# Moving the next to last node batch, and parts of the last one, in the tail of a graph network kernel

## The chip, the cores and the metric

The kernel runs on one core of a Trainium2 chip. A core has five engines, each with its own queue of instructions: TensorE (PE in the profile; its weight loads are listed as PEld), VectorE (DVE), ScalarE (ACT), GpSimd (POOL) and SyncE (SP). They tell each other of finished work by semaphores. Data moves by DMA. Direct transfers are issued by SP, a few by ScalarE; gathers by an index are issued by POOL. The metric is the device time of one execution in microseconds, and lower is better.

## The reference

One layer of a graph network on 6250 nodes with 128 features, and 100000 edges that are sorted by destination. For each edge, the features of both its ends and 4 features of its own go through a small network; its results are summed for each destination node; each node is then updated from its own features and its sum, with two normalizations at the end.

```python
msg_in = concatenate([x[src], x[dst], edge_features], axis=1)
h = silu(msg_in @ mW1 + mb1)
messages = h @ mW2 + mb2
aggregated = segment_sum(messages, dst, num_segments=6250)
u = silu(concatenate([x, aggregated], axis=1) @ uW1 + ub1)
updated = u @ uW2 + ub2
out = layernorm(x + layer_norm(x + updated, ln_g, ln_b))
```

## The kernel before

**Tables.** The first stage multiplies all nodes by the two halves of mW1 and writes two tables to memory, tab_a for sources and tab_b for destinations, so that an edge needs only to add one row of each.

**Groups of edges.** The 100000 edges are cut into 98 groups (NG, numbered 0 to 97) of 1024 (8 tiles of 128); the last group has 6 tiles. For each group g:

- `fetch(g)` has POOL gather the rows of tab_a, one indirect DMA for each tile (line 277), into a buffer ga (six of them). A gather can be made to wait for instructions that are given as further arguments: the first of them holds the first tile, the second the fifth tile. In the steady part these are `begun[g + 2]`, the first matmul of the group's own `products`, and `summing[g]`, the first matmul of the sums of the group two before.
- `load(g)` has SP load 96 rows of tab_b (mv) and the edges' own features (into st).
- `products(g)` makes, on TensorE, the destination part of the first layer in PSUM (pre, line 623).
- `hidden(g)` adds ga and pre on VectorE (s, line 640), and applies Silu on ScalarE (h, line 641).
- `by_nodes(g)` multiplies h by a matrix of zeros and ones, oh (line 609), on TensorE, and so sums the edges of each of 96 nodes in PSUM (pt, line 652).
- `add(g)` adds pt to the sums of all nodes in acc (line 665), and for every fourth group the counts of edges in deg (line 670).

**Batches of nodes.** Sorted edges mean that early nodes are complete before later groups are read. `node_batch` updates four tiles of nodes at a time, as a Python generator: each `yield` ends a step, and `advance` takes every running batch one step further, so that the batches' instructions are strewn among the groups'. The steps are: load x (xs, line 495) and copy the sums; products (y, lines 510, 511 and 515); Silu (uT, line 518); products (lines 521 and 530); residual sum and moments (lines 532, 483 and 484); square root (r, line 489); z and its moments (lines 542 and 545); square root; shift; scaling (line 560); store (line 564). The next to last batch has three tiles of nodes and begins in group 95. The last batch, `final`, has two; it adds the biases to xs early (lines 507 and 508), reads acc and deg directly, and takes its buffers from the pool of the gathers' buffers.

**What sets the order.** The order of each engine's queue is the order in which the Python code issues instructions; nothing is rearranged (the schedule is manual). Semaphore waits are derived from the data. Lines 680 to 722 are the loop over groups: in group g it issues `hidden(g)`, `products(g + 2)`, the matrices of later groups, `by_nodes(g)`, a fetch, adds, and then steps of the batches (line 721: four calls in each of groups 95 and 96). Lines 724 to 759 are the tail: group 97 in two pieces of four and two tiles (`piece`, lines 731 to 734), with `final` around it. A small activation at line 748 ("primed") brings Silu's table back to ScalarE ahead of the pieces, since square root and Silu need different tables.

Of the kernel before, what the change touches and what calls it, by code (L numbers as in the profile page):

```python
# [8 lines left out]
F32 = mybir.dt.float32  # L9
I32 = mybir.dt.int32  # L10
U8 = mybir.dt.uint8
AF = mybir.ActivationFunctionType
# [6 lines left out]
P = 128  # L19
# [5 lines left out]
def kernel(  # L25
# [40 lines left out]
    nc = tc.nc  # L66
    N, H = x.shape
# [4 lines left out]
    G = 8  # L72
    GE = G * P
    NG = -(-E // GE)
# [5 lines left out]
    CLOSE = 14  # L80
# [5 lines left out]
    BT = 4  # L86
# [91 lines left out]
    ones = consts.tile([P, P], F32, name="ones")  # L178
# [94 lines left out]
    def fetch(g, *after):  # L273

        rows[g] = gath.tile([P, G, H], F32, name="ga")
        for i in range(tiles_of(g)):
            ins = nc.gpsimd.indirect_dma_start(  # L277
                out=rows[g][:, i, :],
                out_offset=None,
                in_=x if g < RAW else tab_a[:, :],  # L280
                in_offset=bass.IndirectOffsetOnAxis(
                    ap=src_i[:, g, i : i + 1] if g else src_0[:, i : i + 1], axis=0
                ),
            )
            part, at = divmod(i * len(after), G)
            if after and at == 0 and after[part]:
                tc.add_manual_dep(
                    ins.ins,
                    after[part].ins.name,
                    mybir.DependencyInfo(  # L290
                        mybir.DependencyClass.Sync, mybir.DependencyReason.DATA
                    ),
                    reason="TensorE keeps up with the gathers",
                )
# [124 lines left out]
    def rows_ps():  # L419
        return ps.tile([P, G, P], F32, name="pre")  # L420
# [45 lines left out]
    def node_batch(i0, n, work, new, y, final=False):  # L466

        cols = slice(i0 * P, (i0 + n) * P)
        m = (min((i0 + n) * P, N) - i0 * P) // n
        assert m * n == min((i0 + n) * P, N) - i0 * P  # L470

        def rows_of(t):

            return t[i0 * P : i0 * P + m * n].rearrange("(p j) f -> p j f", j=n)

        def flat(t):
            return t[:, :n].rearrange("p i f -> p (i f)")

        def moments(v):
            mv = work.tile([P, BT, 2], F32, name="mv", bufs=2)  # L480
            for i in range(n):
                st = work.tile([P, 6], F32, name="st", bufs=2)
                nc.vector.bn_stats(st, v[:, i, :])  # L483
                nc.vector.bn_aggr(mv[:, i, :], st)
            return mv

        def std(mv):
            r = work.tile([P, BT], F32, name="r", bufs=2)
            nc.scalar.activation(r[:, :n], mv[:, :n, 1], AF.Sqrt, bias=eps)  # L489
            return r  # L490

        xs = new("xs")
        if m < P:
            nc.vector.memset(xs[m // 32 * 32 :, :n], 0.0)
        nc.sync.dma_start(xs[:m, :n], rows_of(x))
        sums, counts = acc[:, cols], deg[:, cols]
        if not final:

            acc_b, deg_b = new("acc_b"), new("deg_b", DR)
            nc.scalar.copy(flat(acc_b), sums)  # L500
            nc.scalar.copy(flat(deg_b), counts)
            sums, counts = flat(acc_b), flat(deg_b)
        yield
        xb = xs
        if final:
            xb = new("xb")
            nc.vector.tensor_add(xb[:, :n], xs[:, :n], b_b[:, None, :].to_broadcast([P, n, H]))
            nc.vector.tensor_add(xs[:, :n], xs[:, :n], ub2_b[:, None, :].to_broadcast([P, n, H]))
        y = y()
        nc.tensor.matmul(flat(y), u1x, xT[:, cols], start=True, stop=False)  # L510
        nc.tensor.matmul(flat(y), mb2u, counts, start=False, stop=False)  # L511
        if final:

            yield
        nc.tensor.matmul(flat(y), w2u, sums, start=False, stop=True)  # L515
        yield
        uT = new("uT")
        nc.scalar.activation(flat(uT), flat(y), AF.Silu, bias=ub1_col)  # L518
        yield
        if not final:  # L520
            nc.tensor.matmul(  # L521
                y[:, :n],
                ones[0:1, :],
                ub2_row[:, None, :].to_broadcast([1, n, H]),
                start=True,
                stop=False,
            )
        by_p = flat(uT).rearrange("k (p j) -> k p j", j=n)
        for i in range(n):
            nc.tensor.matmul(y[:, i, :], by_p[:, :, i], u2, start=final, stop=final or i == n - 1)  # L530
        yield
        nc.vector.tensor_add(y[:, :n], y[:, :n], xs[:, :n])  # L532
        mv = moments(y)
        if not final:
            nc.vector.tensor_add(xs[:, :n], xs[:, :n], b_b[:, None, :].to_broadcast([P, n, H]))
        yield
        r = std(mv)
        yield
        nc.vector.reciprocal(r[:, :n], r[:, :n])
        z = new("z")  # L540
        for i in range(n):
            nc.vector.scalar_tensor_tensor(
                y[:, i, :], y[:, i, :], mv[:, i, 0:1], g_b, op0=OP.subtract, op1=OP.mult
            )
            nc.vector.scalar_tensor_tensor(
                z[:, i, :], y[:, i, :], r[:, i : i + 1], xb[:, i, :], op0=OP.mult, op1=OP.add
            )
        mz = moments(z)
        yield
        rz = std(mz)  # L550
        yield
        nc.vector.reciprocal(rz[:, :n], rz[:, :n])
        shift = work.tile([P, BT], F32, name="shift", bufs=2)
        nc.vector.scalar_tensor_tensor(
            shift[:, :n], mz[:, :n, 0], -1.0, rz[:, :n], op0=OP.mult, op1=OP.mult
        )
        yield
        o = z
        for i in range(n):
            nc.scalar.activation(  # L560
                o[:, i, :], z[:, i, :], AF.Identity, bias=shift[:, i : i + 1], scale=rz[:, i : i + 1]
            )
        yield
        (nc.scalar if final else nc.sync).dma_start(rows_of(out), o[:m, :n])
# [4 lines left out]
    def advance(running):  # L569

        for b in list(running):
            if next(b, running) is running:
                running.remove(b)
# [106 lines left out]
    for g in range(NG):  # L680
        if g == 1:
            load_weights()
        if g == 2:
            running.append(destination_checks(node_y()))
        if g == 8:
            running.append(fuse_weights())
        for c in range(1, NC):
            if g == max(1, c * EC // GE - 10):
                attributes(c)
            if g == max(1, c * EC // GE - 10) + 1:  # L690
                attribute_rows(c)
        if g + LEAD < NG:
            load(g + LEAD)
        last = g >= NG - 1
        if not last:
            h[g] = hidden(g)
        if g + 2 < NG:
            pre[g + 2] = products(g + 2)
        if g + MADE < NG:
            node_matrix(g + MADE)  # L700
        if g + 1 < NG:
            oh[g + 1] = edge_matrix(g + 1)
        if g - 2 in pt:
            add(g - 2, pt.pop(g - 2))
        if last:
            break
        pt[g] = by_nodes(g, h.pop(g), oh.pop(g))
        if CLOSE <= g + 2 < NG:
            fetch(g + 2, begun[g + 2], summing[g])
        elif g == 0:  # L710
            fetch(7, ended[1], begun[2])
        elif g == 1:
            fetch(8, begun[3], summing[1])
        elif g % 2:
            fetch(g // 2 + 8, ended[g + 1], begun[g + 2] if g == CLOSE - 3 else ended[g + 2])
        if g >= NG - 3:
            add(g - 1, pt.pop(g - 1))
        for i0, n, first in batches[:-1]:
            if g == (first if first >= NG - 3 else first + 1):
                running.append(node_batch(i0, n, *node_tiles(nodes, node_y)))  # L720
        for _ in range(4 if g >= NG - 3 else 2 if g >= NG - 6 else 1):
            advance(running)

    g = NG - 1
    n = tiles_of(g)
    ga, pg, oh_g, h_g = rows.pop(g), pre.pop(g), oh.pop(g), hbuf[g % NH]
    s = work.tile([P, G, H], F32, name="s")
    primed = consts.tile([1, 1], F32, name="primed")
    before = running.pop()

    def piece(lo, hi):
# [1 line left out]
        nc.scalar.activation(h_g[:, lo:hi], s[:, lo:hi], AF.Silu)  # L733
        sums(g, pt[g], h_g, oh_g, lo, hi)

    final = node_batch(
        *batches[-1][:2],
        nodes,

        lambda name, p=P: gath.tile([P, G, H], F32, name="ga")[:p, :BT],  # L740
        lambda: rows_ps()[:, :BT],
        final=True,
    )
    while running:
        advance(running)
    next(final)

    nc.scalar.activation(primed, ones[0:1, 0:1], AF.Silu)
    add(g - 1, pt.pop(g - 1))
    pt[g] = degrees(g)  # L750
    next(final)
# [165 lines left out]
```

## Time and profile before

| what | us |
|---|---|
| median of 3 runs | 1178.11 (1177.94 to 1178.4) |
| profiled execution | 1179.78 |
| its span, first to last instruction | 1177.7 |
| busy: PE, POOL | 747.7, 743.2 |
| busy: PEld, DVE, ACT | 675.3, 486.4, 238.9 |

The profile is of one execution. "Busy" is the time in which an engine works, so that waiting for a semaphore is not in it. In a line of the timeline the columns are start and duration in us, engine, line of the kernel, operation, output and inputs, shapes, how many instructions are merged in the line, and in brackets the idle time before it with what ended it ("remote" is a release that the profile doesn't put down to an instruction). Matmul ends are modelled. An fp32 matmul shows as two records. In a line of the chain of waits the columns are start, duration, and what the time went to. In a group's line stand line, engine, operation and names, then the number of instructions, busy us, mean ns of one, and the idle time before them with its cause.

### The profile page before, as it was taken

The page shows a single profiled execution, that of the slowest core. Times are in us where ns is not written, and L with a number is a line of the kernel's source. Part 1 is how long each engine was busy: PE and PEld are TensorE (multiplying, and loading weights), DVE is VectorE, ACT ScalarE, POOL GpSimd, SP SyncE. Part 2 cuts the span into 40 slices and gives each one's busy share as a digit, 9 for nine tenths or more (in the row PEclk, how much of TensorE's full clock was granted, in tenths as well). Part 3 has the DMA queues.
Part 4 walks back from the last instruction along what each step waited for, and adds up shares of the span by engine and source line. Part 5 has one row for each costly group of instructions (what it writes and reads, how often), then busy time and mean ns, then how long its engine had stood idle before and what let it go on. Part 6 is the DMA issues. An engine that isn't in the chain of part 4 may idle for free.

```text
span 1177.7 us, 11313 instructions
## 1 busy us (share of the span) xinstructions
PE 747.7 (63%) x3645; PEld 675.3 (57%) x3645; DVE 486.4 (41%) x1017; ACT 238.9 (20%) x297; POOL 743.2 (63%) x790
## 2 busy tenths in 40 slices
PE   5776896656756666567647666656566565656654
PEld 4575786555655656465646565555565464656533
DVE  4461654433532523532533353342343252353344
ACT  2211121220321311120221121121132131122132
POOL 6646666665666666666666666666666666656660
PEclk9877877676565666567566667666666667667665
DMA  8762232222222221222222213221222222212110
GB/s 198 203 156 71 75 85 65 67 82 61 74 66 73 67 72 52 79 72 73 55 72 76 58 57 81 65 81 56 71 74 66 71 74 63 65 55 69 47 59 20
DMA packets 70076, 89.01 MB, mean 76 GB/s; under 512 B 20703, under 2 KB 51694, under 8 KB 70010
## 3 DMA queue, kind: packets, MB, share of 16 engines
q0 software_dynamic: 25024, 51.30, 15.8%
q1 hardware_dynamic: 40408, 35.03, 10.3%
q10 hardware_dynamic: 4578, 1.89, 0.7%
q8 instruction: 31, 0.51, 0.2%
q14 instruction: 35, 0.29, 0.1%
HBM read 76.78 MB, written 11.38 MB: 75 GB/s over the span
## 4 chain that ended last, share of the span: by engine, by line
PE 35%; issue 32%; POOL 20%; DVE 2%; DMA 1%; another core or an unknown queue 1%; ACT 1%; DVEq 0%; POOLq 0%; SPq 0%; ACTq 0%
POOL ga L277 20%; PE pre L623 17%; PE pt L652 14%; PE pre L626 1%; PE y L530 1%; DMA ga<-tab_a,src_i 1%; PE y L521 1%; PE y L510 1%; PE y L511 0%; PE y L515 0%; DVE s L640 0%; DVE st L483 0%; DVE oh L609 0%; PE pt L647 0%
## 5 line engine op out<-in xcount | busy, mean ns | idle before, releaser
L277 POOL DMA_INDIRECT ga<-tab_a,src_i x742 | 703.7, 948 | 384.2 <-issue 187.1
L623 PE MATMUL pre<-mv,st 100*128 100x128 f32 x1564 | 345.1, 396 | 229.5 <-issue 199.5
L623 PEld LDWEIGHTS pre<-mv,st 100*128 100x128 f32 x1564 | 315.2, 301 | 248.4 <-issue 224.3
L652 PE MATMUL pt<-oh,h 128*128 128x96 f32 x1564 | 293.7, 348 | 147.6 <-issue 143.8
L652 PEld LDWEIGHTS pt<-oh,h 128*128 128x128 f32 x1564 | 279.9, 266 | 165.8 <-issue 162.3
L640 DVE TENSOR_TENSOR s<-ga,pre 128x1024 f32<-128x1024 f32 x92 | 112.2, 1220 | 502.6 <-DMA ga<-tab_a,src_i 419.8
L641 ACT ACTIVATE h<-s 128x1024 f32<-128x1024 f32 x92 | 97.1, 1056 | 671.5 <-issue 409.6
L596 DVE TENSOR_SCALAR_CACHE_REDUCE st<-near,p_next 96x1024 f32<-96x1024 uint8 x98 | 124.3, 1270 | 2.9 <-DMA near<-near_d 1.5
L609 DVE TENSOR_TENSOR oh<-w_row,rel 128x768 f32<-128x768 f32 x98 | 93.0, 949 | 42.5 <-remote 42.2
L277 POOL DMA_INDIRECT ga<-in_x_dram,src_i x32 | 30.7, 960 | 16.4 <-issue 8.8
L532 DVE TENSOR_TENSOR y<-y,xs 128x512 f32<-128x512 f32 (+1 forms) x12 | 8.3, 688 | 74.4 <-issue 70.7
L641 ACT ACT_TABLE_LOAD x23 | 29.5, 1283 | 24.2 <-PE pre L626 17.6
L489 ACT ACT_TABLE_LOAD x24 | 30.8, 1283 | 6.1 <-DVE st L483 5.7
L377 PE MATMUL wide<-w,xT 128*128 128x256 f32 x98 | 27.6, 441 | 3.5 <-DVE x_sb L380 3.5
L665 DVE TENSOR_TENSOR acc<-acc,pt 128x96 f32 x98 | 23.7, 242 | 12.5 <-PE pt L652 7.7
L530 PEld LDWEIGHTS y<-u,uT 128*128 128x128 f32 x94 | 22.7, 326 | 10.7 <-issue 10.7
L518 ACT ACTIVATE uT<-y,ub_col 128x512 f32<-128x512 f32 (+1 forms) x12 | 8.1, 678 | 96.5 <-remote 83.6
L377 PEld LDWEIGHTS wide<-w,xT 128*128 128x128 f32 x98 | 21.5, 227 | 8.3 <-DVE x_sb L380 4.3
L530 PE MATMUL y<-u,uT 128*128 128x128 f32 x94 | 25.4, 423 | 0.0
L670 DVE TENSOR_TENSOR deg<-deg,pt 1x96 f32 x98 | 24.4, 249 | 1.0
L626 PE MATMUL pre<-w,ga 128*128 128x128 f32 x80 | 19.4, 326 | 2.7 <-issue 2.6
L521 PE MATMUL y<-ub_row,ones 1*128 1x512 f32 (+1 forms) x24 | 15.5, 729 | 6.9 <-ACT uT L518 6.9
(118 smaller groups left out, 361.7 us busy)
## 6 DMA issues: line engine op xcount, KB each, us to landing
ga<-tab_a,src_i POOLq DMA_INDIRECT x742
near<-near_d SPq DMA_DIRECT2D x24, 384.0 KB
mv<-tab_b SPq DMA_DIRECT2D x98, 48.0 KB
tab_a<-t SPq DMA_DIRECT2D x6, 512.0 KB
tab_b<-x_sb SPq DMA_DIRECT2D x6, 512.0 KB
xs<-in_x_dram SPq DMA_DIRECT2D x11, 256.0 KB
out_dram<-z SPq DMA_DIRECT2D x11, 256.0 KB
st<-ea_d SPq DMA_DIRECT2D x98, 16.0 KB
```

What stands on the lines that cost most here:

```text
L277: ins = nc.gpsimd.indirect_dma_start(out=rows[g][:, i, :], out_offset=None, in_=x if g < RAW else tab_a[:, :], in_offset=bass.IndirectOffs ...
L377: ins = nc.tensor.matmul(pm[:, j], xT[:, cols], w1, start=True, stop=True)
L489: nc.scalar.activation(r[:, :n], mv[:, :n, 1], AF.Sqrt, bias=eps)
L521: nc.tensor.matmul(y[:, :n], ones[0:1, :], ub2_row[:, None, :].to_broadcast([1, n, H]), start=True, stop=False,)
L530: nc.tensor.matmul(y[:, i, :], by_p[:, :, i], u2, start=final, stop=final or i == n - 1)
L596: nc.vector.tensor_scalar(stbuf[g % NST][:W], near.pop(g), p_next, 0.0, op0=OP.is_equal, op1=OP.add, accum_out=deg_q[g // DQ % 2][:, g % D ...
L609: nc.vector.tensor_tensor(oh, w_row[:, None, :].to_broadcast([P, G, W]), rel[:, g, :, None].to_broadcast([P, G, W]), op=OP.is_equal,)
L623: ins = nc.tensor.matmul(pre[:, i, :], st[:, i, :], mv[g % NM], start=True, stop=g >= RAW)
L626: ins = nc.tensor.matmul(pre[:, i, :], rows[g][:, i, :], w1[:, 0, :], start=False, stop=True)
L640: nc.vector.tensor_add(s[:, :n], ga[:, :n], ps[:, :n])
L641: nc.scalar.activation(h[:, :n], s[:, :n], AF.Silu)
L652: ins = nc.tensor.matmul(pt[:, :W], h[:, i, :], oh[:, i, :], start=i == 0, stop=i == tiles_of(g) - 1)
```

## The change

There are three parts.

1. In group 96 the four steps of the next to last batch are issued at the head of the group, ahead of `hidden(96)`, and no longer at its end.
2. `final` is made at the end of group 95 and takes its first step there (memset and load of xs). Its second step is issued at the end of group 96; a new `yield` ends this step after the first product (line 510), and the product with the counts (line 511) follows with group 97 after its `degrees`. The small activation at line 748 is gone.
3. The six gathers of group 97 are issued by `fetch(g + 2)` without further arguments, so they don't wait for `begun[97]` and `summing[95]`. All other groups keep theirs.

```diff
         nc.tensor.matmul(flat(y), u1x, xT[:, cols], start=True, stop=False)
+        if final:
+            yield
         nc.tensor.matmul(flat(y), mb2u, counts, start=False, stop=False)
 ...
         last = g >= NG - 1
+        if g == NG - 2:
+            for _ in range(4):
+                advance(running)
         if not last:
             h[g] = hidden(g)
 ...
-        if CLOSE <= g + 2 < NG:
+        if CLOSE <= g + 2 < NG - 1:
             fetch(g + 2, begun[g + 2], summing[g])
+        elif g + 2 == NG - 1:
+            fetch(g + 2)
 ...
-        for _ in range(4 if g >= NG - 3 else 2 if g >= NG - 6 else 1):
+        for _ in range(0 if g == NG - 2 else 4 if g == NG - 3 else 2 if g >= NG - 6 else 1):
             advance(running)
+        if g == NG - 3:
+            final = node_batch(
+                *batches[-1][:2],
+                nodes,
+                lambda name, p=P: gath.tile([P, G, H], F32, name="ga")[:p, :BT],
+                lambda: rows_ps()[:, :BT],
+                final=True,
+            )
+            next(final)
+        if g == NG - 2:
+            next(final)
 ...
-    primed = consts.tile([1, 1], F32, name="primed")
 ...
-    final = node_batch(
-        ...
-    )
     while running:
         advance(running)
-    next(final)
-
-    nc.scalar.activation(primed, ones[0:1, 0:1], AF.Silu)
     add(g - 1, pt.pop(g - 1))
     pt[g] = degrees(g)
     next(final)
```

More of the change, by code (lines that the diff above doesn't have):

```diff
@@ L734, in piece @@
         sums(g, pt[g], h_g, oh_g, lo, hi)
-    final = node_batch(
[L737 to L742, printed above, removed]
-    )
     while running:
         advance(running)
-    next(final)
-    nc.scalar.activation(primed, ones[0:1, 0:1], AF.Silu)
     add(g - 1, pt.pop(g - 1))
```

## The prediction

> **What bounds the kernel now.** I read the page from top to bottom, then the chain of waits and the timeline of the last 60 us, because the change begins in group 95 of 0 to 97.
>
> ```profile
> span 1177.7 us, 11313 instructions
> PE 747.7 (63%) x3645; PEld 675.3 (57%) x3645; DVE 486.4 (41%) x1017; ACT 238.9 (20%) x297; POOL 743.2 (63%) x790
> ...
> L277 POOL DMA_INDIRECT ga<-tab_a,src_i x742 | 703.7, 948 | 384.2 <-issue 187.1
> ```
>
> No engine is full. Most of the run is the gathers' rhythm: one starts every 1.25 us (0.95 busy, 0.30 idle), and now and then POOL stands still until TensorE reports. The change leaves all that alone up to about 1137 us. What follows is a tail, and the chain of waits tells what sets it:
>
> ```profile
> 1138.37 7.42 another core or an unknown queue
> ...
> 1145.87 0.59 ACT uT L518
> 1146.46 0.04 issue
> 1146.50 1.64 PE y L521 x2
> 1148.14 1.59 PE y L530 x6
> ...
> 1156.08 2.08 DMA ga<-in_x_dram
> ...
> 1160.58 2.89 PE pt L652 x12
> ```
>
> The chain runs through the next to last node batch, then the load of the last batch, then the two pieces of group 97. The 7.42 us without a name are the largest single piece. The timeline shows what they are:
>
> ```profile
> 1139.13 0.48 PE L515 MATMUL y<-acc_b,w2u 128*128 128x384 f32 x1 [1.03 <-issue]
> ...
> 1145.80 0.26 DVE L665 TENSOR_TENSOR acc<-acc,pt 128x96 f32 x1 [4.80 <-remote]
> 1145.82 0.94 POOL L277 DMA_INDIRECT ga<-tab_a,src_i  x1 [2.46 <-remote]
> 1145.87 0.58 ACT L518 ACTIVATE uT<-y,ub_col 128x384 f32<-128x384 f32 x1 [7.50 <-remote]
> ```
>
> TensorE's last product of that batch ends at 1139.61 by its record. VectorE, GpSimd and ScalarE all wait for TensorE (for pt of group 95, for its first product, for y), and all three start within 0.07 us at 1145.8. So TensorE's signals come up to 6 us later than its records, in one burst. The timeline of POOL gives a hint on when:
>
> ```profile
> 1100.80 0.95 POOL L277 DMA_INDIRECT ga<-tab_a,src_i  x1 [0.30 <-issue]
> 1105.17 0.94 POOL L277 DMA_INDIRECT ga<-tab_a,src_i  x1 [3.43 <-remote]
> ```
>
> From 176 us on POOL stops 45 times for more than 1 us; 37 of these stops last 3.23 to 3.62 us, the other eight 1.33 to 2.82. A wait for a varying amount of TensorE work would not be so constant. It looks as if the burst comes a fixed time after the last gather, whatever TensorE does: before 1145.8 TensorE had been idle for 6 us.
>
> [...]
>
> **Part 1: the next to last batch goes ahead of the rows of group 96.** The instruction lists of both kernels show the same work on TensorE in the same order. On VectorE and ScalarE the order changes: VectorE does y L532, the moments, z and its moments first, and only then s of group 96, oh of group 97 and acc of group 95. ScalarE does both square roots before h of group 96. This is what is moved, with its place before:
>
> ```profile
> 1138.92 1.22 DVE L640 TENSOR_TENSOR s<-ga,pre 128x1024 f32<-128x1024 f32 x1 [2.77 <-DMA ga<-tab_a,src_i]
> ...
> 1146.35 1.04 ACT L641 ACTIVATE h<-s 128x1024 f32<-128x1024 f32 x1
> ...
> 1149.67 3.62 PE L652 MATMUL pt<-oh,h 128*128 128x96 f32 x16
> ...
> 1155.48 0.18 DVE L484 BATCH_NORM_AGGREGATE mv<-st 128x2 f32<-128x6 f32 x1
> ...
> 1159.17 1.02 DVE L732 TENSOR_TENSOR s<-ga,pre 128x512 f32<-128x512 f32 x2
> ```
>
> Before, s was made in the dead time before 1145.8, h behind uT, and pt of group 96 ran under VectorE's work on the batch (1149.8 to 1155.66): all hidden. After, VectorE waits at y L532 with s behind it, so s, h and pt come one after another behind 1155.66. With the batch's own times unchanged: s 1155.7 to 1156.9. ScalarE: root to 1156.06, Silu's table 1.28 to 1157.36, so h 1157.37 plus 1.05 gives 1158.42 (the table, not s, decides). pt 3.62 at half clock and 0.05 to start: 1162.1. acc and the two deg additions take 0.67 (1156.08 to 1156.75 before): group 97's s starts at 1162.8 or 1162.9. It was 1159.17: **plus 3.7**. From there to the end all stays (s to acc L665 was 1163.49 - 1159.17 = 4.32), so the end moves by 3.7.
>
> What hides beside it: oh (0.95), acc of 95 (0.25), L507 and L508 (0.9) fit between 1156.8 and 1162.1 on VectorE. L510 and L511 (1.1 and 1.2 us) lie behind pt on TensorE; L511 waits for deg at 1162.8 and is done at about 1164.0, when h of the first piece comes at 1162.85 + 0.72 + 0.69 = 1164.3. If that cover goes, up to 1.2 more. If pt ran at full clock (0.11 instead of 0.22 us apart), 1.8 less. Part 1: 1.9 to 4.9.
>
> **Part 2: last batch's load and first products in front.** The memset (0.27) and the load (2.08) leave the chain behind 1155.66, L507 and L508 too. That is already in the 3.7: VectorE's wait of 1.50 for the load is gone, but VectorE would be waiting for pt then. By itself 0 now; it would have been worth about 3 with s of 96 where it was. The load's place in SP's queue is the same, behind one store; it can start near 1139 among the last gathers and isn't needed before 1157. The added yield only splits L510 from L511: 0. Removing the priming activation saves its 0.20 on ScalarE, off the path; its table load remains, now ahead of h of 96.
>
> **Part 3: the last six gathers no longer wait for TensorE.** POOL now waits only for its queue and for VectorE's read of the buffer's old rows, long done. Two stops go, 1.33 - 0.30 and 2.46 - 0.30, so the gathers start at 1137.64, 1138.89 and on to 1143.89, and end at 1144.84 rather than 1148.02. Their rows were used at 1159.17, so the 3.2 us buy nothing. But if the burst comes a fixed time after the last gather, it now comes later: before, POOL had gone quiet at 1143.37 (because it waited) and the burst came 2.46 later; now it goes quiet at 1144.84, and 2.46 to 3.5 later is 1147.3 to 1148.3 against 1145.82. **Plus 1.5 to 2.5; I take 2.0.** y, and all that follows, waits for it. No row of before shows this directly. Its bounds: nothing if the burst has another cause, and minus 6.1 if the waits themselves held the signals (1145.87 back to 1139.7).
>
> **Sum.** 3.7 + 0 + 2.0 = 5.7. The profiled span goes from 1177.7 to 1183.4, its execution from 1179.78 to 1185.5. The median shown, 1178.11, lies 1.67 below the profiled execution; with the same distance the median is **1183.8**, 0.5% slower.
>
> **Rivals.**
> A, the forecast: order plus a later burst. From 1.9 + 1.5 to 4.9 + 2.5: 1181.5 to 1185.5. For it: the constant stops, and the idle TensorE. Chance 0.54.
> B: the burst doesn't care for gathers; only the order counts, 1178.1 + 3.7 = 1181.8. For it: a steady rhythm of two groups could make constant stops by itself. Against: TensorE idle from 1139.6 on. 0.23.
> C, the other side: the held signals are due to POOL waiting on TensorE. Without those waits y arrives up to 6.1 us sooner, the order's 3.7 stays, and the time is 1178.1 - 2.4 = 1175.7. It decides from where y comes before 1142.1 (1145.8 less 3.7). Against: signals are also late through whole stretches in which POOL doesn't wait (1122.64 to 1137.33; acc L665 of group 94 started at 1135.61, 9.5 us after its products' records). 0.08.
> D: the change pays for itself: s of 96 is cheaper than I think because something I book behind 1155.66 overlaps, and the result is within noise, 1178 to 1180.4. Against: the order on VectorE is fixed in the list. 0.07.
> E: the burst comes later still, or L510 and L511 push the pieces: above 1185.5. 0.08.
> That the change does not do what it says is excluded by the lists: the six gathers' two waits on TensorE are gone and the orders are as told.
>
> **Numbers.** 0.2% is 2.4 us, about what this measurement can tell from no change. Slower than 1180.5: A, B, E, 0.85. Within: D, and half of C, 0.11. Faster than 1175.75: the other half, 0.04. The likeliest is A at 1183.8 with its own range 1181.5 to 1185.5. The whole range reaches down into D and up into E: 1179.5 to 1186.5.
>
> **What will show it.** In the profile after: POOL's last six gathers 1.25 us apart and over near 1145; uT L518 of the next to last batch starting at 1147.3 to 1148.3 (A) or at 1145.9 (B) or before 1142 (C); VectorE idle until y L532; s L640 of group 96 within 0.2 us behind the last L484 of that batch, ScalarE's table load between the second root and h; pt L652 of group 96 about 2.8 us behind that L484; and 11.5 us rather than 7.8 from that L484 to the last acc L665. I'd be wrong if pt of 96 were still made under the batch's VectorE work, or if the burst came while gathers ran.

## The result, and the profile after

| | before | after |
|---|---|---|
| median of 6 runs, us | 1178.26 (1176.51 to 1179.82) | 1183.56 (1183.27 to 1185.62) |
| profiled execution, us | 1179.78 | 1183.55 |
| its span, us | 1177.7 | 1181.7 |

The ratio is 1.0049, with an interval of 1.0036 to 1.0062: the changed kernel is slower by half a per cent, some 5.3 us. The new code moves the line numbers: L640 is now L643, L652 is L655, L665 is L668, and L515 and L518 are L518 and L521.

The page of the changed kernel first, with the head, the engines' busy time and the group of gathers:

```profile
span 1181.7 us, 11309 instructions
...
PE 737.9 (62%) x3645; PEld 667.3 (56%) x3645; DVE 486.4 (41%) x1017; ACT 238.8 (20%) x296; POOL 741.1 (63%) x790
...
L277 POOL DMA_INDIRECT ga<-tab_a,src_i x742 | 701.8, 946 | 382.8 <-issue 200.5
```

The work is the same as before; only ScalarE has one instruction less. The gathers take 701.8 us (703.7 before) and POOL's idle time ahead of them 382.8 (384.2). So the difference is not in the steady part, and the end of the chain of waits has to show it:

```profile
1138.24 10.14 another core or an unknown queue
...
1148.47 0.59 ACT uT L521
1149.06 3.36 issue
...
1158.68 1.28 ACT L644
1159.97 1.07 ACT h L644
...
1161.08 3.74 PE pt L655 x16
```

Two things are new. The piece without a name, which starts within 0.13 us of where it did before, lasts 10.14 us and not 7.42. And Silu's table load (1.28 us), h and pt of group 96 now stand in the chain; before, they ran beside it. The timeline of the changed kernel has the instructions themselves:

```profile
1139.01 0.48 PE L518 MATMUL y<-acc_b,w2u 128*128 128x384 f32 x1 [1.03 <-issue]
...
1143.78 0.94 POOL L277 DMA_INDIRECT ga<-tab_a,src_i  x1 [0.30 <-issue]
...
1148.47 0.58 ACT L521 ACTIVATE uT<-y,ub_col 128x384 f32<-128x384 f32 x1 [10.22 <-remote]
...
1152.42 0.57 DVE L535 TENSOR_TENSOR y<-y,xs 128x384 f32<-128x384 f32 x1 [16.02 <-issue]
...
1158.09 0.18 DVE L484 BATCH_NORM_AGGREGATE mv<-st 128x2 f32<-128x6 f32 x1
1158.36 0.30 ACT L489 ACTIVATE r<-mv,eps 128x3 f32<-128x3 f32 x1 [3.70 <-DVE mv L484]
1158.46 1.22 DVE L643 TENSOR_TENSOR s<-ga,pre 128x1024 f32<-128x1024 f32 x1 [0.19 <-issue]
1158.68 1.28 ACT L644 ACT_TABLE_LOAD   x1
...
1165.55 1.02 DVE L752 TENSOR_TENSOR s<-ga,pre 128x512 f32<-128x512 f32 x2
1166.95 1.58 PE L655 MATMUL pt<-oh,h 128*128 128x96 f32 x12 [0.68 <-ACT h L753]
1168.57 0.25 DVE L668 TENSOR_TENSOR acc<-acc,pt 128x96 f32 x1 [2.00 <-PE pt L655]
1170.14 0.74 PE L533 MATMUL pre<-u,ga 128*128 128x128 f32 x4 [0.56 <-ACT ga L521]
```

The last gather starts at 1143.78 and the gathers no longer pause. The product y was recorded as done at 1139.49, but uT, which reads it, did not start before 1148.47. VectorE did nothing for 16.02 us ahead of L535, with s of group 96 (L643) queued behind that instruction. After the last L484 come s, the table load, h, pt (3.73 us) and only then the pieces of group 97 at 1165.55. The tail in parts, from these rows and those of before, of which two more are needed here:

```profile
1163.49 0.26 DVE L665 TENSOR_TENSOR acc<-acc,pt 128x96 f32 x1 [3.30 <-PE pt L652]
...
1165.59 1.22 PE L530 MATMUL pre<-u,ga 128*128 128x128 f32 x4 [0.56 <-ACT ga L518]
```

| stretch | before | after | difference |
|---|---|---|---|
| start of uT of the next to last batch | 1145.87 | 1148.47 | +2.60 |
| uT to the end of its last L484 | 9.79 | 9.80 | +0.01 |
| end of L484 to the start of the pieces' s | 3.51 | 7.28 | +3.77 |
| s of the pieces to the start of the last acc | 4.32 | 3.02 | -1.30 |
| start of the last acc to the end of the span | 14.21 | 13.13 | -1.08 |
| sum | | | +4.00 |

The last two rows are gains that I had not foreseen. In both, TensorE ran at a higher clock: the pieces' six products (twelve records) took 1.58 us (2.88 before), and the two products of L533 (four records) took 0.74 (1.22). The windows view gives a granted clock of 0.50 for all of 1146 to 1178 before. After, it gives 0.50 from 1146 to 1165, so for pt of group 96 too, then 0.99 from 1165 to 1168.8 and 1.00 from 1168.8 to 1171.

### The profile page after: what moved, and what is told of

Same layout as the page of the kernel before. It is cut to its first block, busy times and chain, and to the rows that moved or that the text cites. A ratio compares the mean times of both kernels' runs of the same rounds, so it can differ in the third digit from the quotient of the medians.

```text
span 1181.7 us, 11309 instructions
## 1 busy us (share of the span) xinstructions
PE 737.9 (62%) x3645; PEld 667.3 (56%) x3645; DVE 486.4 (41%) x1017; ACT 238.8 (20%) x296; POOL 741.1 (63%) x790
## 4 chain that ended last, share of the span: by engine, by line
issue 19%; POOL 14%; PE 13%; DVE 2%; another core or an unknown queue 2%; DMA 1%; ACT 1%; DVEq 0%; POOLq 0%; ACTq 0%
POOL ga L277 14%; PE pre L626 6%; PE pt L655 5%; DMA ga<-tab_a,src_i 1%; PE y L533 0%; DVE z L548 0%; DVE y L545 0%; DVE oh L612 0%; DVE st L483 0%; ACT z L563 0%; DVE mv L484 0%; DVE s L643 0%; DVE st L599 0%; PE y L524 0%
## 5 line engine op out<-in xcount | busy, mean ns | idle before, releaser
L277 POOL DMA_INDIRECT ga<-tab_a,src_i x742 | 701.8, 946 | 382.8 <-issue 200.5
L626 PE MATMUL pre<-mv,st 100*128 100x128 f32 x1564 | 340.1, 392 | 248.0 <-issue 225.7
L626 PEld LDWEIGHTS pre<-mv,st 100*128 100x128 f32 x1564 | 310.5, 297 | 269.9 <-issue 256.0
L655 PE MATMUL pt<-oh,h 128*128 128x96 f32 x1564 | 290.6, 345 | 141.3 <-issue 130.6
L655 PEld LDWEIGHTS pt<-oh,h 128*128 128x128 f32 x1564 | 276.9, 264 | 157.6 <-issue 146.9
L643 DVE TENSOR_TENSOR s<-ga,pre 128x1024 f32<-128x1024 f32 x92 | 112.3, 1221 | 504.3 <-DMA ga<-tab_a,src_i 441.0
L535 DVE TENSOR_TENSOR y<-y,xs 128x512 f32<-128x512 f32 (+1 forms) x12 | 8.3, 689 | 81.9 <-issue 81.9
L644 ACT ACT_TABLE_LOAD x24 | 30.8, 1283 | 24.6 <-PE pre L629 17.7
L489 ACT ACT_TABLE_LOAD x24 | 30.8, 1283 | 6.1 <-DVE mv L484 5.7
L533 PEld LDWEIGHTS y<-u,uT 128*128 128x128 f32 x94 | 22.7, 327 | 10.3 <-issue 10.3
L668 DVE TENSOR_TENSOR acc<-acc,pt 128x96 f32 x98 | 23.7, 242 | 9.7 <-PE pt L655 5.3
L521 ACT ACTIVATE uT<-y,ub_col 128x512 f32<-128x512 f32 (+1 forms) x12 | 8.1, 678 | 92.4 <-remote 59.3
L533 PE MATMUL y<-u,uT 128*128 128x128 f32 x94 | 25.4, 422 | 0.0
```

What stands on the lines that cost most here:

```text
L277: ins = nc.gpsimd.indirect_dma_start(out=rows[g][:, i, :], out_offset=None, in_=x if g < RAW else tab_a[:, :], in_offset=bass.IndirectOffs ...
L626: ins = nc.tensor.matmul(pre[:, i, :], st[:, i, :], mv[g % NM], start=True, stop=g >= RAW)
L643: nc.vector.tensor_add(s[:, :n], ga[:, :n], ps[:, :n])
L644: nc.scalar.activation(h[:, :n], s[:, :n], AF.Silu)
L655: ins = nc.tensor.matmul(pt[:, :W], h[:, i, :], oh[:, i, :], start=i == 0, stop=i == tiles_of(g) - 1)
L668: nc.vector.tensor_add(at, at, pt[:, :W])
```

## Experiments

The theory is A: the order costs about 3.7 us, and TensorE's signals come later because the gathers end later. The rivals are B (only the order costs) and C (POOL's waits on TensorE hold the signals, so removing them brings y sooner). All experiments but one ran where the kernel before takes about 1013 us, and where TensorE's signals are not held up while gathers run: in nine of their timelines uT starts 0.09 or 0.10 us behind the record of y's last product, against 6.26 in the first profile of before. Two, the run with four more gathers and the last one with held gathers, are put here by their times alone. Only the run with eight more gathers found them held, as in the first profiles (1178.51 us for the kernel before). So the order could be priced in several runs, and the burst only in one.

How different the two conditions are is seen in the page of the first experiment, which but for the last group's waits is the kernel before:

```profile
span 1013.0 us, 11312 instructions
...
L277 POOL DMA_INDIRECT ga<-tab_a,src_i x742 | 701.4, 945 | 232.8 <-issue 209.4
```

The gathers take as long as in the first profiles, 701.4 us; what is gone is 151 of the 384.2 us of POOL's idle time. In the profile of before, the pauses of over 0.5 us ahead of gathers, less the usual 0.30 each, add up to 166 us; here the 232.8 us over 742 gathers are 0.31 each, about the usual pause.

### Part 3 alone

```diff
-        if CLOSE <= g + 2 < NG:
+        if CLOSE <= g + 2 < NG - 1:
             fetch(g + 2, begun[g + 2], summing[g])
+        elif g + 2 == NG - 1:
+            fetch(g + 2)
```

> The kernel before, with only the last six gathers freed from their waits for TensorE. A (TensorE's signals are held until some 2.5 to 3.7 us after the last gather): uT of the next to last batch starts at about 1148.4 instead of 1145.9, and the end moves by the same 2.6 us, to about 1180.8. B (the burst does not care for gathers): uT stays at 1145.9, time as before, 1178.2. C (POOL's waits hold the signals): uT before 1142, time below 1175.

Measured: 1014.4 us against 1013.85, ratio 1.0001 (0.9992 to 1.001). The timeline of this run:

```profile
981.55 0.81 PE L515 MATMUL y<-acc_b,w2u 128*128 128x384 f32 x2
982.42 1.22 DVE L640 TENSOR_TENSOR s<-ga,pre 128x1024 f32<-128x1024 f32 x1 [6.81 <-DMA ga<-tab_a,src_i]
982.46 0.58 ACT L518 ACTIVATE uT<-y,ub_col 128x384 f32<-128x384 f32 x1 [3.73 <-PE y L515]
983.42 0.95 POOL L277 DMA_INDIRECT ga<-tab_a,src_i  x1 [0.30 <-issue]
...
985.17 1.95 PE L652 MATMUL pt<-oh,h 128*128 128x96 f32 x16
...
994.67 1.02 DVE L734 TENSOR_TENSOR s<-ga,pre 128x512 f32<-128x512 f32 x2
...
998.99 0.26 DVE L665 TENSOR_TENSOR acc<-acc,pt 128x96 f32 x1 [3.30 <-PE pt L652]
```

Here uT starts 0.10 us behind the end of L515's record, although gathers still start at 983.42 and later. There is nothing for a burst to delay, and part 3 is worth nothing, neither a loss nor C's gain.

### Parts 1 and 2, without part 3

The changed kernel with the waits of the last gathers put back:

```diff
-        if CLOSE <= g + 2 < NG - 1:
+        if CLOSE <= g + 2 < NG:
             fetch(g + 2, begun[g + 2], summing[g])
-        elif g + 2 == NG - 1:
-            fetch(g + 2)
```

> The changed kernel, but the last six gathers wait for TensorE as before. A: uT is back at 1145.9, and only the order costs: from the end of the batch's last moments (L484) to the last acc stays at about 10.3 us as in the changed kernel (7.8 before), time about 1180.8, 2.6 under the changed kernel. B: uT stays at about 1148.4 as in the changed kernel, since something else in the order brought it there, and the time stays at 1183.5.

Measured: 1017.09 us, ratio 1.0032 (1.0024 to 1.0041), which is 3.2 us. Its timeline:

```profile
980.11 0.58 ACT L521 ACTIVATE uT<-y,ub_col 128x384 f32<-128x384 f32 x1 [2.41 <-PE y L518]
...
989.04 1.22 DVE L643 TENSOR_TENSOR s<-ga,pre 128x1024 f32<-128x1024 f32 x1 [0.19 <-DMA ga<-tab_a,src_i]
...
991.66 3.73 PE L655 MATMUL pt<-oh,h 128*128 128x96 f32 x16 [8.68 <-ACT h L644]
...
997.52 1.58 PE L655 MATMUL pt<-oh,h 128*128 128x96 f32 x12 [0.24 <-ACT h L751]
999.14 0.26 DVE L668 TENSOR_TENSOR acc<-acc,pt 128x96 f32 x1 [2.00 <-PE pt L655]
```

From uT to the last acc it is 19.03 us, and 16.53 in the run before: s of group 96 has moved from beside uT to 8.93 us behind it, and TensorE stood idle for 8.68 us ahead of pt. From the last L484 to the last acc it is 10.29 us, as expected. This profiled execution (1014.41 us) is one of the shortest of its 20 (1014.29 to 1020.13), so its tail need not be that of the median.

### Part 1 alone, and part 2 alone

Part 1 alone:

```diff
+        if g == NG - 2:
+            for _ in range(4):
+                advance(running)
         if not last:
             h[g] = hidden(g)
 ...
-        for _ in range(4 if g >= NG - 3 else 2 if g >= NG - 6 else 1):
+        for _ in range(0 if g == NG - 2 else 4 if g == NG - 3 else 2 if g >= NG - 6 else 1):
```

> Only part 1: the next to last batch ahead of the rows of group 96; the last batch's load, steps and small activation as before. Both theories: the order's price of parts 1 and 2 together (3.2 us in run 2) plus L507 and L508 (0.85), which now follow the load behind acc and deg: about 4 us slower. If part 2 were what costs, part 1 alone would be the same as before or faster.

Measured: 1019.46 us against 1014.19, ratio 1.0043 (1.0024 to 1.0063). From uT to the last acc it took 21.24 us, 4.7 more than with the order of before. The pieces' products took 2.87 us here, and in the run of parts 1 and 2 1.58.

Part 2 alone is the changed kernel with its waits and with the batch's steps back at the end of group 96:

```diff
-        if g == NG - 2:
-            for _ in range(4):
-                advance(running)
 ...
-        for _ in range(0 if g == NG - 2 else 4 if g == NG - 3 else 2 if g >= NG - 6 else 1):
+        for _ in range(4 if g >= NG - 3 else 2 if g >= NG - 6 else 1):
```

> Only the last batch's load and first steps ahead; the next to last batch behind the rows of group 96, and the gathers with waits, as before. Both theories: the load of 2.08 us leaves the chain, VectorE goes from the moments (end 1155.66) over L507, L508, acc and deg (0.9 and 0.67) to the pieces at about 1157.3 instead of 1159.17, so about 1.9 us faster, 1176.3. If part 2 is worth nothing without part 1, 1178.2.

Measured: 1011.43 us, ratio 0.9975 (0.9968 to 0.9982): faster than the kernel before, by 2.4 us, and no version was better clear of noise; it was not run where signals are held. Its timeline:

```profile
979.49 0.58 ACT L521 ACTIVATE uT<-y,ub_col 128x384 f32<-128x384 f32 x1 [3.03 <-PE y L518]
980.33 1.22 DVE L643 TENSOR_TENSOR s<-ga,pre 128x1024 f32<-128x1024 f32 x1 [6.62 <-DMA ga<-tab_a,src_i]
982.75 3.09 PE L655 MATMUL pt<-oh,h 128*128 128x96 f32 x16 [0.40 <-ACT h L644]
...
989.72 1.02 DVE L746 TENSOR_TENSOR s<-ga,pre 128x512 f32<-128x512 f32 x2
...
994.04 0.26 DVE L668 TENSOR_TENSOR acc<-acc,pt 128x96 f32 x1 [3.30 <-PE pt L655]
```

With s of group 96 beside uT and pt under the batch, the early load does pay: uT to the last acc is 14.55 us, 2.0 less than with part 3 alone. By the medians part 1 costs 5.3 us and part 2 gains 2.4, which gives 2.9; together they cost 3.2. By the ratios it is 0.43% less 0.25%, against 0.32%. Within these intervals the two parts add up.

### Part 2 with its biases later

In the profile of part 2 alone the pieces' s could start earlier if L507 and L508 didn't stand ahead of it, so I issued them ahead of `final`'s last product.

```diff
-        if final:
-            xb = new("xb")
-            nc.vector.tensor_add(xb[:, :n], xs[:, :n], b_b[...])
-            nc.vector.tensor_add(xs[:, :n], xs[:, :n], ub2_b[...])
 ...
+        if final:
+            xb = new("xb")
+            nc.vector.tensor_add(xb[:, :n], xs[:, :n], b_b[...])
+            nc.vector.tensor_add(xs[:, :n], xs[:, :n], ub2_b[...])
         nc.tensor.matmul(flat(y), w2u, sums, start=False, stop=True)
```

> Part 2 alone, and the last batch's two bias additions (L507 and L508, 0.85 us) moved behind the pieces and the last acc, where VectorE waits for TensorE anyway. Without held signals: ScalarE's Silu table (1.28 us behind the second root) now decides when the first piece's h starts, so 0.4 us of the 0.85 remain: 0.28 to 0.3% under the kernel before. With held signals the same way, 2.3 us under the kernel before.

Measured: 1011.53 us, ratio 0.9983 (0.9974 to 0.9991). Faster than before, but no better than part 2 alone, so the expectation was missed. The timeline shows what was late next:

```profile
988.29 1.28 ACT L747 ACT_TABLE_LOAD   x1
988.53 1.02 DVE L746 TENSOR_TENSOR s<-ga,pre 128x512 f32<-128x512 f32 x2
989.58 0.93 ACT L747 ACTIVATE h<-s 128x512 f32<-128x512 f32 x2
```

The first half of s is made long before h can start, since Silu's table is loaded until 989.57. In the run of part 2 alone the table was there at 990.03 and h waited for s until 990.44, so 0.41 us was the most that this edit could bring, as expected. From the last L484 to the last acc that gain is there: 5.30 us, and 5.70 with part 2 alone. But from uT to that L484 the batch took 9.34 us, and 8.85 with part 2 alone, since s of group 96 got its gathers 1.33 us behind uT and not 0.84. So uT to the last acc is 14.64 us, against 14.55, and a step of 0.4 us is less than the two medians can tell apart.

### The gathers held back until the batch's product

If the signals come when the gathers have stopped, then gathers that wait for y's last product would let y through sooner. The same edit was made on the kernel before, on part 2 and on the changed kernel:

```diff
+        made[i0] = nc.tensor.matmul(flat(y), w2u, sums, start=False, stop=True)
 ...
+        elif g + 2 == NG - 1:
+            pass
 ...
+        if g == NG - 3:
+            fetch(g + 2, made[batches[-2][0]])
```

> The kernel before, but the first of the last six gathers waits for the next to last batch's last product into y (L515 of the kernel before), so that POOL is quiet from 1137.3 on. A: the burst comes 2.5 to 3.7 us later, uT starts at 1140 to 1141 instead of 1145.9, and the end comes some 5 us sooner, about 1173. The gathers then run from about 1140.5 to 1148, before their rows are used. B: uT stays at 1145.9 and the time at 1178.2, or is longer, because the gathers start later. C: the one stop is now a wait for TensorE, so signals are held at least as long: 1178 or more.

> Part 2 alone (the better version so far), and the first of the last six gathers waits for the next to last batch's last product into y. With held signals, A: uT at 1140 to 1141 and the load off the chain, together 5 to 7 us under the kernel before; B: 2 us under it. Without held signals: as part 2 alone, 2.4 us (0.25%) under the kernel before, or 0.5 better.

> The changed kernel, but the last six gathers wait for the next to last batch's last product into y. With held signals, A: uT at 1140 to 1141 instead of 1148.5, and 7 us under the changed kernel (1176); B: 1183.5 as the changed kernel. Without held signals: as the changed kernel, 0.3% over the kernel before.

> The kernel of run 4 (the first of the last six gathers waits for the next to last batch's last product into y), for a chip on which TensorE's signals are held. A: POOL goes quiet at about 1137, the burst comes 2.5 to 4.8 us later, uT of the next to last batch starts at 1140 to 1142 instead of 1145.9, and the time is 4 to 6 us under the kernel before, 1172 to 1174.5. B: uT at 1145.9 and the time as before, 1178.5. On a chip without held signals: as in run 4, 0.1% under the kernel before.

Measured, each against the kernel before: 1013.11 us with the hold alone, ratio 0.9991 (0.9985 to 0.9998); 1011.49 with part 2, 0.9973 (0.9962 to 0.9984); 1016.59 with the changed kernel, 1.0022 (1.0005 to 1.0039); and, with the hold alone once more, a single 1012.18 against 1012.13. All four ran where signals aren't held, so they say nothing on A. They do say that a start of the last gathers that is later by some 0.6 to 1.6 us costs nothing there: the same parts without the hold gave 0.9975 and 1.0032, and the intervals overlap. Whether the hold would help where signals are held stays open.

The run on the changed kernel shows one thing more. It has the changed kernel's order, but these are its pieces:

```profile
998.06 1.02 DVE L756 TENSOR_TENSOR s<-ga,pre 128x512 f32<-128x512 f32 x2
...
999.46 2.87 PE L657 MATMUL pt<-oh,h 128*128 128x96 f32 x12 [0.16 <-ACT h L757]
1002.37 0.26 DVE L670 TENSOR_TENSOR acc<-acc,pt 128x96 f32 x1 [3.30 <-PE pt L657]
```

The pieces' products took 2.87 us, as long as at the granted clock of 0.50 before (2.88), though TensorE had been at work until 0.16 us ahead of them. From their s to the last acc it is 4.31 us, as in the kernel before, and from uT to the last acc 20.32, which is 3.8 more than with part 3 alone. In the profiled execution of parts 1 and 2, with the pieces' products in 1.58 us, it was 2.5 more.

### The whole change where signals aren't held

The changed kernel, unedited.

> The changed kernel once more, beside the kernel before. On a chip where TensorE's signals come at once (as in runs 1 to 4, where the kernel before takes 1013.9 us and POOL never stops): A and B both expect only the order's price, as in run 2, 0.3% (about 3.2 us), since part 3 alone made no difference there. On a chip with held signals (1178 us): A 5.3 us, as in the result.

Measured: 1016.56 us against 1014.19, ratio 1.0032 (1.0018 to 1.0046). That is what parts 1 and 2 cost without part 3. So where no signal is held the order is the whole of the loss, as B has it.

### More gathers at the end

Part 3 alone, and behind the last group's gathers four more, then eight more, into a spare buffer that nobody reads. They add no work to any other engine; they only keep the gathers going 5 or 10 us longer (1.25 us each).

```diff
         elif g + 2 == NG - 1:
             fetch(g + 2)
+            for i in range(8):
+                nc.gpsimd.indirect_dma_start(
+                    out=spare[:, i % 4, :],
+                    out_offset=None,
+                    in_=tab_a[:, :],
+                    in_offset=bass.IndirectOffsetOnAxis(ap=src_i[:, g, i : i + 1], axis=0),
+                )
```

> Part 3 alone, and behind the last six gathers four more of the same rows into a tile that nobody reads, so that POOL stays busy 5 us longer. With held signals, A: uT of the next to last batch starts 5 us later than with part 3 alone, at about 1153.4, and the end moves with it, to about 1186; B: nothing moves, since nobody waits for these rows. Without held signals both expect no more than 0.5 us.

> Part 3 alone, and eight more gathers behind the last six, so that POOL gathers to within some 10 us of the end. With held signals, A: uT of the next to last batch starts about 10 us later than with part 3 alone, near 1158, and the span ends 10 us later. Without held signals (POOL never stops for TensorE in the steady part): uT follows its last product within 0.6 us as in run 1, and the span moves by less than 2 us; if gathers as such held TensorE's signals on every chip, uT would start only after the last of them.

Four more, where signals aren't held: 1013.9 us, ratio 1.0000 (0.9993 to 1.0007). There the gathers by themselves cost nothing.

Eight more, where signals are held: 1192.28 us against 1178.51, one run each. The timeline of this run:

```profile
1134.99 0.26 DVE L666 TENSOR_TENSOR acc<-acc,pt 128x96 f32 x1 [4.96 <-PE pt L653]
1135.16 0.95 POOL L277 DMA_INDIRECT ga<-tab_a,src_i  x1 [0.30 <-issue]
...
1142.03 0.80 PE L515 MATMUL y<-acc_b,w2u 128*128 128x384 f32 x1 [2.34 <-issue]
1142.67 0.94 POOL L277 DMA_INDIRECT ga<-tab_a,src_i  x1 [0.31 <-issue]
...
1152.67 0.95 POOL L714 DMA_INDIRECT spare<-tab_a,src_i  x1 [0.30 <-issue]
1158.38 0.26 DVE L666 TENSOR_TENSOR acc<-acc,pt 128x96 f32 x1 [18.44 <-remote]
1158.44 0.58 ACT L518 ACTIVATE uT<-y,ub_col 128x384 f32<-128x384 f32 x1 [20.69 <-remote]
```

TensorE's product y is recorded as done at 1142.83. ScalarE gets it 15.6 us later, 4.8 us after the last of the useless gathers. Against the first profile of before, uT is later by 12.57 us (1158.44 against 1145.87) and the span is longer by 12.8 (1190.5 against 1177.7): the delay goes through to the end undiminished. Against the profile of the changed kernel, which has part 3 too, uT is later by 9.97 us (1158.44 against 1148.47), and eight gathers take 10.0. B had uT unmoved. So y's signal came behind the gathers, and gathers added there cost their time even if nobody needs their rows; this rests on one run.

It is not so for every signal. In the kernel before and in the changed kernel the acc of group 94 starts at 1135.61 and 1135.48, behind records that end at 1126.09 and 1126.22: its signal came 9.52 and 9.26 us late, but in the midst of gathers that run without a pause from 1122.64 to 1137.33 before, and from 1122.57 to 1144.72 after. With eight more gathers the acc at 1134.99 is that of group 94, and gathers run on past it. With part 3 alone, where signals aren't held, VectorE was not idle at all ahead of that acc (974.72). What lets one signal through and holds the next is not known.

## Why the prediction was right

The forecast was 1183.8 us, the median 1183.56. That the two are so close is luck: the profiled execution was forecast at 1185.5 and was 1183.55, 1.95 less, but the forecast then took off 1.67 for the distance between profiled execution and median, and after the change there was no such distance. The mechanism, order plus a later burst, is what the runs show. Point by point:

- **The burst (part 3, +2.0, from 1.5 to 2.5).** Right in kind, and a little small: uT came 2.60 us later, at 1148.47, just past the 1147.3 to 1148.3 that were named. The eight useless gathers moved uT by their own time, so at this place the gathers' end decides. What was wrong is the fixed distance of 2.46 to 3.5 us from the end of the gathers: it was 2.46 before (from POOL's going quiet at 1143.37), 3.75 after (last gather over at 1144.72), and 4.8 with eight more. I know of no row that fixes it. That end of the gathers was as expected (1144.84). Nor does the end of the gathers decide for every signal: the prediction named a burst while gathers run as a sign against itself, and the acc at 1135.61, which it used against C alone, is such a release.
- **The order (part 1, +3.7).** Its working up to the pieces holds: +3.77 in the profile. s starts 0.19 us behind the last L484, the table decides h (loaded until 1159.96, h at 1159.97, s ready at 1159.68), pt starts 2.81 us behind L484 and takes 3.73 us. That VectorE would sit idle until L535 is seen too (16.02 us).
- **"From there to the end all stays".** This is the step that missed. It was booked at 0 and is -2.4 in the profiled execution (-1.30 and -1.08), nearly all of it from TensorE's clock (0.50 before, 0.99 and 1.00 after): 1.30 in the pieces' products, 0.52 in those of L518 and 0.48 in those of L533. I had considered full clock for pt of group 96 (the lower end of part 1; it took 3.73 us at 0.50), and not for what follows it. So 11.5 us from the last L484 to the last acc were expected, and 10.3 came. Over the whole tail the profile gives +4.0, and the forecast sum was 5.7. The medians differ by 5.3, because the profiled execution of before lay 1.5 us above the median of its six runs; how often the pieces' products take 1.58 us is not known beyond the profiled executions. With held gathers the same order had them in 2.87 us, and there this step held (4.31 against 4.32, and 3.8 for the order).
- **Part 2, "0 now, about 3 with s of 96 where it was".** Alone it gains 2.4 us where signals aren't held, about as said; the load and the biases leave the chain. The 0 was a way of booking: the 3.7 of part 1 was worked out with part 2 in place. Without part 2 the tail of part 1 was 2.2 us longer (21.24 against 19.03): 0.9 up to the pieces' s, where L507 and L508 then stand in the chain, and 1.3 from the pieces' products (2.87 against 1.58).
- **C** fell. With the waits gone, uT was later by 2.60 us where signals are held, and where they aren't the waits' removal changed nothing (1.0001).
- **B** holds only where signals aren't held: there the change costs the order alone, 1.0032. The remainder to 1.0049 fits part 3's burst, but the two intervals (1.0018 to 1.0046 and 1.0036 to 1.0062) overlap, so the size of part 3 rests on the profile's 2.60 us and not on these ratios.

Whether a held signal is due to the gathers' writes or to something else about the gathers was not tried. What decides whether signals are held stays open too. That it is a lasting trait of a chip is not shown: the run with eight more gathers and the last one with held gathers, a few minutes later, are both listed under chip 1, and the kernel before took 1178.51 us beside the one and 1012.13 beside the other. Whether that number means one and the same chip is not known.

## What to carry to other kernels

When work of a late batch is moved ahead of a group's rows, look at what stands behind its first waiting instruction on VectorE: here the work that had filled a wait moved to the end of it (16.02 us), and s, h and pt came one after another, at a cost of 3.77 us. Price the parts of a change apart, as the early load alone gained 0.25% and the reordering alone cost 0.43% (both where signals aren't held). And when a consumer starts long after its producer's record, measure on what the signal waits, by adding useless work of one suspect, before removing or adding waits.

## What the runs showed of the hardware

One kernel took 1178 us in some runs and 1013 us in others. In the slower ones TensorE's work is recorded as done and its consumers start much later: with eight more gathers uT started 15.6 us behind the record of y, and acc of group 95 23.9 us behind the records of its products (end 1134.51, start 1158.38). In the steady part of the profile of before 37 of POOL's stops last 3.23 to 3.62 us; the first experiment's page has 0.31 us ahead of a gather in the mean, and from 969.69 to 987.17 none over 0.31.

The page of the profile before has 24 table loads of ScalarE at the square root (L489) and 23 at Silu (L641), each of 1283 ns.

TensorE's pace in the tail differed between executions of the same order. With pt of group 96 and the next products ahead of the pieces, the pieces' products took 1.58 us in the changed kernel, with and without held signals, and in parts 1 and 2; in the first profile of the changed kernel the granted clock was 1.00 there (1166.9 to 1168.6). They took 2.87 us with held gathers and with part 1 alone, as they did with the order of before (2.87 or 2.88; 0.50 in the first profile of before). TensorE's pause straight ahead of them was 0.68, 0.23 and 0.24 us where they took 1.58, and 0.16 and 1.07 us where they took 2.87. No run here shows what decides it.
